# A selective scan with four states of 32 channels in the partitions: dt and dt x through DRAM, y summed in four column groups, two PSUM banks for projections

## The chip, the cores and the metric

The kernel runs on one core of a Trainium2 chip. The core has engines that work side by side, each through its own list of instructions in order: PE (TensorE) multiplies matrices, DVE (VectorE) and POOL (GpSimd) work element by element, ACT (ScalarE) evaluates functions, SP (SyncE) issues most DMA transfers. Semaphores make one engine wait for another. SBUF has 128 partitions; matmuls write into PSUM, which has eight banks of 128 partitions by 2 KB (512 numbers of 32 bits). DRAM lies outside and is reached by DMA alone.

The metric is the device time of one execution in microseconds (us); lower is better.

## The reference, cut to what matters

Two layers on x of shape (2, 2048, 256). Layer 0 adds causal attention and a mixture of experts with a gate; layer 1 adds a selective state-space branch (Mamba) and a linear map with a ternary weight. The change concerns layer 1 and the gate that ends layer 0:

```python
g = sigmoid(concat([abel, moe @ rot]) @ mix_w + mix_b)       # the gate, one number a token
x = residual + abel * (1 - g) + (moe @ rot) * g              # with the attention's share added
xn = layernorm(x)
xs, z = split(xn @ in_proj_w.T, 2)                           # 512 channels each
xs = silu(conv1d(xs, 4 taps) + conv_b)
dt, Bm, C = split(xs @ x_proj_w.T, [16, 32])                 # 16, 16 and 16 wide
dt = softplus(dt @ dt_proj_w.T + dt_proj_b)                  # 512 channels
for t in range(2048):                                        # per channel d and state n (16 states)
    h[d, n] = exp(dt[t, d] * A[d, n]) * h[d, n] + dt[t, d] * Bm[t, n] * xs[t, d]
    y[t, d] = sum_n h[d, n] * C[t, n]
out = x + ((y + xs * D) * silu(z)) @ out_proj_w.T + xn @ ternary(weight).T * alpha + bias
```

The recurrence holds 2 batch rows times 512 channels times 16 states, each a chain of 2048 steps.

## The kernel before, in words

Layer 0 fills the first 2.17 ms or so: projections, attention, routing, `experts`. `rotation`, drawn on beside the experts, computes `rot` and, with `mix_w`, the vector `rw` = rot · mix_w (256 numbers, repeated in all partitions) for the gate. `sab` holds the abel part of the gate, one number a token. Layer 1 and the gate are in `mix_and_state_space`.

The sequence is cut into four chunks of `CH` = 512 tokens; a unit is one chunk of one batch row, eight units in the order (chunk, row). Within a unit the 512 channels lie as `NB` = 4 blocks of 128 in the partitions, with 512 tokens in the free dimension.

The recurrence of a unit runs over 16 states `n`. `product(n)` (L1502 on) loads row n of B and C from DRAM (`bc_d`), repeated over 128 partitions (512 KB), copies B to PSUM on ACT (`bb`, L1507) and multiplies `uh = dx * bb` on DVE (L1509), where `dx` is dt times x. Then for each block m: ACT computes `da = exp(dt * a)` with one `a` a partition (L1526), and DVE runs one scan instruction over the 512 tokens (L1527), started from `carry`. After the four, POOL stores the last column as `carry` (L1532) and multiplies `hh *= C` (L1533). `summed` adds the state's `hh` to `y` on PE with the identity as weights (L1514), into four PSUM banks (`ps_y`) over all 16 states; it is issued for the state before.

Other work of a unit is written as three generators that the recurrence advances at listed places (`places`, pairs of state and block):
- `ahead` of the next unit: normalise (`n`, L1279), transpose (`tr`), project (`in`, L1176), convolve by four diagonal matmuls a block (`cv`, L1316, evacuated as `xs` by ACT, L1325), Silu (L1432), x projection (`xp`), `bc_d` written to DRAM, dt projection, softplus in pieces on ACT, DVE (L1378, L1383) and POOL (L1381), and `dx` (POOL, L1385).
- `behind`: `leave` of the unit before (output projection `out`, L1398 to L1403, added into `xc` by DVE at L1413, stored), then `gate` of this unit (`z` projection, Silu). `gated` for the unit before, at state 1, computes `xs + D` terms with y (DVE, L1460) and multiplies by `zs` (POOL, L1465).
- `mix` of the unit after next: gathers each token's two expert rows (`ys`, POOL's indirect DMA, L1196), scales them on ACT (L1205), adds them (POOL, L1211), multiplies by `rw` (POOL, L1214), reduces on DVE and forms the gate `g` (L1218 to L1224), turns the rows (`moT`), multiplies by `rot` (`pn`, L1241, added by DVE at L1248), adds abel's share on POOL (L1257), and takes the statistics and `r`, `nm` (L1263 to L1270).

`mm`, `issued` and `settle` share one PSUM bank (`ps_m`) among the projections: a matmul group's evacuation is held back and emitted when the next group asks for the bank. `ps_a` has three banks for `da` and `bb`.

The text of the program is not the order of the engines: a scheduler arranges the instructions of each engine by its own estimate of when they are due, and each engine then executes its list in that fixed order. SP's DMA issues stand in such a list too, and one whose source isn't ready holds up those behind it.

Of the kernel before, what the change touches and what calls it, by code (L numbers as in the profile page):

```python
# [19 lines left out]
P = 128  # L20
B = 2
S = 2048
D = 256
# [76 lines left out]
def tile_model(ctx: ExitStack, tc: tile.TileContext, t, out):  # L100
# [54 lines left out]
    rw = keep.tile([P, D], F32, name="rw")  # L155
# [290 lines left out]
def rotation(tc, t, row, ident, ones, pool, ps_pool, tag, rot, rw):  # L446
# [38 lines left out]
    ps = ps_pool.tile([P, D], F32, tag=tag, name="rw_ps")  # L485
    for k in range(2):
        nc.tensor.matmul(
            ps,
            lhsT=mw[:, k : k + 1].to_broadcast([P, P]),
            rhs=turned[:, k, :],  # L490
            start=(k == 0),
            stop=(k == 1),
        )
# [592 lines left out]
def mix_and_state_space(tc, t, col, row, ident, ones, rot, routes, sab, rw, y_d, ab_d, xa_d, out_tiles):  # L1086
# [6 lines left out]

    nc = tc.nc
    NC = S // CH
    QT = CH // P
    full = [P, NB, CH]
    with ExitStack() as ctx:
# [3 lines left out]
        bcp = ctx.enter_context(tc.tile_pool(name="ss_bc", bufs=3))  # L1102
        wk = ctx.enter_context(tc.tile_pool(name="ss_k", bufs=2))
        xcp = ctx.enter_context(tc.tile_pool(name="ss_x", bufs=4))
        dr = ctx.enter_context(tc.tile_pool(name="ss_d", bufs=2, space=DRAM))
        ps_y = ctx.enter_context(tc.tile_pool(name="ss_py", bufs=1, space=PSUM))
        ps_a = ctx.enter_context(tc.tile_pool(name="ss_pa", bufs=3, space=PSUM))
        ps_m = ctx.enter_context(tc.tile_pool(name="ss_pm", bufs=1, space=PSUM))
# [9 lines left out]
        a_neg = w.tile([P, NB * DS], F32, name="a_neg")  # L1118
        nc.scalar.activation(a_neg, col("a_log"), AF.Exp)
        nc.vector.tensor_scalar(a_neg, a_neg, -1.0, None, ALU.mult)  # L1120

# [9 lines left out]
        nc.vector.tensor_scalar(nmb, row("mix_b"), -1.0, None, ALU.mult)  # L1131

# [18 lines left out]
        for b in range(B):  # L1151
            cr = w.tile([P, DS, NB], F32, name=f"carry{b}")
            nc.gpsimd.memset(cr, 0.0)
            carry.append(cr)
            tl = w.tile([P, NB, DC - 1], F32, name=f"tail{b}")
            nc.gpsimd.memset(tl, 0.0)
            tail.append(tl)
# [3 lines left out]
        def settle():  # L1161
            if held:
                take, ps = held.pop()
                take(ps)

        def mm(name, shape=(P, CH)):
            settle()
            return ps_m.tile(list(shape), F32, tag="mm", name=name)

        def issued(ps, take):  # L1170
            held.append((take, ps))
# [13 lines left out]
        def mix(c, b, m_):  # L1185

            u = f"{b}_{c}"
            n0 = (b * NC + c) * QT
            ys = one.tile([P, TOP, QT, D], F32, tag="ys", name=f"ys_{u}")
            ab = one.tile([P, QT, D], F32, tag="ab", name=f"ab_{u}")  # L1190
            nc.sync.dma_start(ab, ab_d[:, n0 : n0 + QT, :])
            xc = m_["xc"] = xcp.tile([P, QT, D], F32, tag="xc", name=f"xc_{u}")
            nc.sync.dma_start(xc, xa_d[:, n0 : n0 + QT, :])
            for i in range(QT):
                for e in range(TOP):
# [6 lines left out]
                    yield  # L1202
            for e in range(TOP):
# [4 lines left out]
                if e == 0:  # L1208
                    yield
# [3 lines left out]

            nc.gpsimd.tensor_tensor(  # L1214
                ys[:, 1], mo, rw.unsqueeze(1).to_broadcast([P, QT, D]), ALU.mult
            )
            g = one.tile([P, 2, QT], F32, tag="g", bufs=2, name=f"g_{u}")
            nc.vector.tensor_reduce(g[:, 0, :], ys[:, 1], AX.X, ALU.add)  # L1218
            nc.vector.tensor_tensor(g[:, 0, :], g[:, 0, :], sab[:, n0 : n0 + QT], ALU.add)
            nc.scalar.activation(g[:, 0, :], g[:, 0, :], AF.Exp, scale=-1.0, bias=nmb)  # L1220
            yield
            nc.vector.tensor_scalar(g[:, 1, :], g[:, 0, :], 1.0, None, ALU.add)
            nc.vector.reciprocal(g[:, 0, :], g[:, 1, :])
            nc.vector.tensor_scalar(g[:, 1, :], g[:, 0, :], -1.0, 1.0, ALU.mult, ALU.add)  # L1224

            moT = ys[:, 1].rearrange("p (k i) d -> p k (i d)", k=2)
            for k in range(2):
# [6 lines left out]
                yield  # L1234
            settle()
# [18 lines left out]
            settle()  # L1254
            for i in range(QT):
                nc.scalar.activation(ab[:, i, :], ab[:, i, :], AF.Copy, scale=g[:, 1, i : i + 1])
            nc.gpsimd.tensor_tensor(xc, xc, ab, ALU.add)  # L1257
# [7 lines left out]
            r = m_["r"] = one.tile([P, QT], F32, tag="r", bufs=3, name=f"r3_{u}")  # L1265
            nc.vector.tensor_scalar(r, mv[:, :, 1], EPS, None, ALU.add)
            nc.scalar.activation(r, r, AF.Sqrt)
            nc.vector.reciprocal(r, r)
            nm = m_["nm"] = one.tile([P, QT], F32, tag="nm", bufs=3, name=f"nm3_{u}")
            nc.vector.scalar_tensor_tensor(nm, mv[:, :, 0], -1.0, r, ALU.mult, ALU.mult)  # L1270
            yield

        def norm(c, b, m_):

            u = f"{b}_{c}"

            n3 = one.tile([P, QT, D], F32, tag="k", name=f"n3_{u}")
            for i in range(QT):
# [4 lines left out]
                    scale=m_["r"][:, i : i + 1],  # L1283
# [23 lines left out]
            m_["xr"] = xr  # L1307

        def convolve(c, b, m_):
            u = f"{b}_{c}"  # L1310
            xr = m_["xr"]
# [19 lines left out]
            nc.gpsimd.tensor_copy(tail[b], xr[:, :, CH:])  # L1331

        def before2(c, b, m_):

            u = f"{b}_{c}"
            xs = m_["xs"]
# [7 lines left out]
            bc_d = m_["bc_d"] = dr.tile([2 * DS, CH], F32, tag="bc_d", name=f"bc_d_{u}")  # L1344

            def out_of(ps):
                nc.scalar.copy(xp, ps)
                nc.sync.dma_start(bc_d, xp[DR:, :])
# [4 lines left out]
            dt = m_["dt"] = two.tile(full, F32, tag="dt", name=f"dt_{u}")  # L1353
# [15 lines left out]
            dx = m_["dx"] = two.tile(full, F32, tag="dx", name=f"dx_{u}")  # L1369
            s1, s2 = dx, one.tile(full, F32, tag="k", name=f"s2_{u}")  # L1370
# [7 lines left out]
            nc.vector.scalar_tensor_tensor(s1, s2, 1.0, s1, ALU.subtract, ALU.subtract)  # L1378
            nc.scalar.activation(s2, s2, AF.Ln)
            yield  # L1380
            nc.gpsimd.tensor_tensor(s2, s2, s1, ALU.subtract)  # L1381
            yield
            nc.vector.scalar_tensor_tensor(dt, dt, 0.0, s2, ALU.max, ALU.add)  # L1383
            yield
            nc.gpsimd.tensor_tensor(dx, dt, xs, ALU.mult)  # L1385
            yield

        def leave(c, b, m_):

            u = f"{b}_{c}"  # L1390
            n0 = (b * NC + c) * QT
            xnT, zs, xc = m_["xnT"], m_["zs"], m_["xc"]
            for h in range(2):
                ps = mm(f"out_{u}_{h}", (P, 2, D))
# [24 lines left out]
        def gate(c, b, m_):  # L1419

            zs = m_["zs"] = one.tile(full, F32, tag="zs", name=f"zs_{b}_{c}")
            for m in range(NB):
# [3 lines left out]
                )  # L1426
                yield
            settle()

        def silu(*tiles):  # L1430
            for x in tiles:
                nc.scalar.activation(x, x, AF.Silu)  # L1432
            yield
# [4 lines left out]
        def ahead(at):  # L1438

            u, m_ = units[at], of[at]  # L1440
            yield from norm(*u, m_)
            yield from convolve(*u, m_)
            yield from silu(m_["xs"])
            yield from before2(*u, m_)

        def behind(at):

            if at > 0:
                yield from leave(*units[at - 1], of[at - 1])
            else:  # L1450
                yield
                yield
            yield from gate(*units[at], of[at])
            yield from silu(of[at]["zs"])

        def gated(m_, pieces):

            xs, y, zs = m_["xs"], m_["y"], m_["zs"]
            for m in range(NB):
# [21 lines left out]
        for kind, at in enumerate(kinds):  # L1481
            for p in at:
                places.setdefault(p, []).append(kind)
# [158 lines left out]
```

## Time and profile before

| | |
|---|---|
| median of three runs | 3504.89 us (3504.43 to 3509.85) |
| profiled execution | 3507.69 us, span 3506.0 us |
| busy share of the span | PE 86%, DVE 63%, ACT 48%, PEld 48%, POOL 32% |
| mean granted PE clock | 0.926 |
| first `uh` of unit 0 | 2271.80 us |
| end of the last scan | 3472.8 us |
| DMA moved | 289.70 MB, mean 83 GB/s |

The profile lists one execution. A row of the groups gives line, engine, operation, output and inputs with their shapes and how many there were; then busy time and the mean duration in ns; then the time that the engine was idle just before them, with what released it. PE runs an fp32 matmul as two passes, so it shows two records for each matmul of the program. PEld is the loading of weights, which overlaps PE. A table by stretches gives each engine's busy time in a window, the granted PE clock (1.0 is full speed) and the share and rate of DMA.

### The profile page before, as it was taken

The page shows a single profiled execution, that of the slowest core. Times are in us where ns is not written, and L with a number is a line of the kernel's source. Part 1 is how long each engine was busy: PE and PEld are TensorE (multiplying, and loading weights), DVE is VectorE, ACT ScalarE, POOL GpSimd, SP SyncE. Part 2 cuts the span into 40 slices and gives each one's busy share as a digit, 9 for nine tenths or more (in the row PEclk, how much of TensorE's full clock was granted, in tenths as well). Part 3 has the DMA queues.
Part 4 walks back from the last instruction along what each step waited for, and adds up shares of the span by engine and source line. Part 5 has one row for each costly group of instructions (what it writes and reads, how often), then busy time and mean ns, then how long its engine had stood idle before and what let it go on. Part 6 is the DMA issues. An engine that isn't in the chain of part 4 may idle for free.

```text
span 3506.0 us, 40686 instructions
## 1 busy us (share of the span) xinstructions
PE 2999.4 (86%) x15574; PEld 1686.0 (48%) x15574; DVE 2218.6 (63%) x2927; ACT 1690.8 (48%) x2423; POOL 1139.4 (32%) x834
## 2 busy tenths in 40 slices
PE   7878899999999998999999995486868787787867
PEld 4633344444444444888888883132423342333423
DVE  6576677777777774331111111298989798889896
ACT  4434455555555554223323323465556565565543
POOL 4223301000100011110010003267566666656664
PEclk9978899999999998999999997697989898888988
DMA  8823213122221104334444431122222222322221
GB/s 296 229 69 79 77 25 49 25 43 37 36 38 25 25 1 154 129 135 146 138 137 145 141 120 45 37 61 68 69 73 67 67 69 65 84 55 60 67 66 48
DMA packets 123874, 289.70 MB, mean 83 GB/s; under 512 B 14464, under 2 KB 57488, under 8 KB 109472
## 3 DMA queue, kind: packets, MB, share of 16 engines
q1 hardware_dynamic: 104960, 187.37, 21.7%
q0 software_dynamic: 17376, 98.58, 8.2%
q8 instruction: 123, 2.02, 0.3%
q10 hardware_dynamic: 1344, 1.16, 0.1%
q14 instruction: 71, 0.58, 0.1%
HBM read 224.13 MB, written 62.91 MB: 82 GB/s over the span
## 4 chain that ended last, share of the span: by engine, by line
PE 49%; DVE 23%; POOL 10%; issue 8%; ACT 7%; DMA 3%; DVEq 0%; POOLq 0%; ACTq 0%; SPq 0%
DVE hh L1527 10%; PE h L1050 8%; PE o L1063 8%; PE pv L661 7%; PE s L703 7%; PE m L606 5%; POOL hh L1533 4%; DVE best L619 4%; DVE uh L1509 4%; PE q L354 3%; PE cv L1316 2%; ACT p L711 2%; DMA x_d<-rows,slots 2%; PE po L751 1%; ACT da L1526 1%
## 5 line engine op out<-in xcount | busy, mean ns | idle before, releaser
L619 DVE TENSOR_REDUCE best<-m 128x2 f32<-128x1024 f32 (+3 forms) x640 | 677.5, 1064 | 161.5 <-PE m L606 152.5
L711 ACT ACTIVATE p<-s 128x1024 f32<-128x1024 f32 (+3 forms) x640 | 573.9, 897 | 418.0 <-PE s L703 399.7
L1527 DVE TENSOR_TENSOR_SCAN hh<-da,carry,uh 128x512 f32<-128x512 f32 x512 | 619.7, 1264 | 84.2 <-PE y L1514 52.5
L1514 PE MATMUL y<-hh,ident 128*128 128x512 f32 x1024 | 531.6, 656 | 86.6 <-POOL hh L1533 68.1
L1533 POOL TENSOR_TENSOR hh<-hh,bc 128x2048 f32<-128x2048 f32 x128 | 579.3, 4526 | 10.4 <-POOL carry L1532 0.2
L1526 ACT ACTIVATE da<-dt,a_neg 128x512 f32<-128x512 f32 x512 | 351.0, 689 | 340.7 <-DVE hh L1527 224.6
L661 PE MATMUL pv<-p,v 128*17 128x256 f32 (+1 forms) x4608 | 412.1, 379 | 46.7 <-POOL p L716 41.9
L716 POOL TENSOR_SCALAR_AFFINE_SELECT p<-p 128x256 f32<-128x256 f32 x256 | 104.6, 410 | 907.4 <-ACT p L711 907.0
L1514 PEld LDWEIGHTS y<-hh,ident 128*128 128x128 f32 x1024 | 205.2, 208 | 363.4 <-issue 235.3
L606 PE MATMUL m<-k,q 64*128 64x512 f32 (+3 forms) x1280 | 322.4, 466 | 9.2 <-DVE best L619 8.4
L703 PE MATMUL s<-q,k 64*128 64x512 f32 (+3 forms) x1280 | 284.9, 410 | 33.2 <-DVE best L619 30.4
L1050 PE MATMUL h<-xT,w 128*128 128x256 f32 x1248 | 294.2, 382 | 1.1 <-DVE xT L1038 1.1
L1057 ACT ACTIVATE hT<-h,b1s 128x256 f32<-128x256 f32 x312 | 142.3, 471 | 314.1 <-PE h L1050 314.1
L1509 DVE TENSOR_TENSOR uh<-dx,bb 128x2048 f32<-128x2048 f32 x128 | 289.4, 2261 | 5.6 <-POOL dx L1385 4.6
L1063 PE MATMUL o<-w,hT 128*128 128x256 f32 x1248 | 280.3, 379 | 0.0
L1020 POOL DMA_INDIRECT w<-in_w,wrow x78 | 76.3, 978 | 621.5 <-PE h L1050 354.1
L703 PE MATMUL s<-tops,onesr 64*128 64x512 f32 (+3 forms) x1280 | 266.9, 379 | 0.0
L606 PEld LDWEIGHTS m<-k,q 64*128 64x128 f32 x1280 | 131.5, 188 | 264.7 <-PE s L703 142.3
L1050 PEld LDWEIGHTS h<-xT,w 128*128 128x128 f32 x1248 | 233.5, 191 | 33.4 <-DVE xT L1038 3.6
L1063 PEld LDWEIGHTS o<-w,hT 128*128 128x128 f32 x1248 | 233.4, 190 | 30.8
L1078 DVE COPY yt<-o 128x512 f32<-128x512 f32 x39 | 27.0, 691 | 336.7 <-PE o L1070 336.7
L661 PEld LDWEIGHTS pv<-p,v 128*17 128x17 f32 x4608 | 86.9, 95 | 246.2 <-POOL p L716 91.6
(298 smaller groups left out, 3690.4 us busy)
## 6 DMA issues: line engine op xcount, KB each, us to landing
bc<-bc_d SPq DMA_DIRECT2D x128, 512.0 KB, 4.9
q<-qk_d SPq DMA_DIRECT2D x128, 128.0 KB, 4.2
k<-qk_d SPq DMA_DIRECT2D x128, 128.0 KB, 7.2
x_d<-zero SPq DMA_DIRECT2D x6, 1664.0 KB
xg<-x_d SPq DMA_DIRECT2D x39, 256.0 KB, 2.8
y_d<-yt SPq DMA_DIRECT2D x39, 256.0 KB
qk_d<-qp SPq DMA_DIRECT2D x16, 512.0 KB, 7.3
qk_d<-kp SPq DMA_DIRECT2D x16, 512.0 KB, 3.9
```

The lines of the kernel that those rows point to most:

```text
L606: nc.tensor.matmul(ps[:, h, 0:n], lhsT=qT[hs, qs], rhs=kT[hs, c * CH : c * CH + n], start=True, stop=True, tile_position=(HP * h, 0),)
L619: nc.vector.tensor_reduce(best[:, i, :, c], ps[:, :, 0:n], AX.X, ALU.max)
L661: nc.tensor.matmul(pv[r0 : r0 + HS + 1, 0, lo - f * HC : HC], lhsT=v[:, b * TPB + kb, 2 * pr + h, :], rhs=pt[:, h, lo:hi], start=False, st ...
L703: nc.tensor.matmul(ps[:, h, off:CH], lhsT=(kT[hs, kb * P : (kb + 1) * P], onesr[hs, :])[i], rhs=(qT[hs, j * CH + off : (j + 1) * CH], tp[h ...
L711: nc.scalar.activation(pt[:, :, off:CH], ps[:, :, off:CH], AF.Exp, scale=float(HS) ** -0.5)
L1050: nc.tensor.matmul(ph, lhsT=w1[:, k * DF + f * P : k * DF + (f + 1) * P], rhs=xT[:, k, :], start=(k == 0), stop=(k == 1),)
L1063: nc.tensor.matmul(po[:, h, :], lhsT=hT[:, f, h * P : (h + 1) * P], rhs=w2[:, f * D : (f + 1) * D], start=(f == 0), stop=False,)
L1509: nc.vector.tensor_tensor(uh, dx, bb.to_broadcast(full), ALU.mult)
L1514: nc.tensor.matmul(y[:, m, :], lhsT=ident, rhs=hh[:, m, :], start=(n == 0), stop=(n == DS - 1))
L1526: nc.scalar.activation(da, dt[:, m, :], AF.Exp, scale=a_neg[:, k : k + 1])
L1527: nc.vector.tensor_tensor_scan(hh[:, m, :], da, uh[:, m, :], carry[b][:, n, m : m + 1], ALU.mult, ALU.add)
L1533: nc.gpsimd.tensor_tensor(hh, hh, cn, ALU.mult)
```

## The change

In the recurrence the 128 partitions hold four states of 32 channels in place of one state of 128 channels. A group (m, g) has channel block m and the states 4g to 4g+3; there are 16 groups (`NU`) a unit, walked block by block, each with four scans, one for each quarter q of the block's channels. So:
- `dt` and dt times x go to DRAM (`dd_d`) in eight DMAs a unit (`spill`) and come back per block m, repeated for the four states, by `decays`: four DMAs of 32 partitions, 512 KB each, into one of two `dd` buffers. Blocks 1 to 3 are asked for while the block before is worked on, block 0 of the next unit at group 14.
- B and C are loaded per g in four DMAs of 32 partitions (`b_and_c`), four times a unit instead of 16; each load serves all four blocks.
- `a_neg` is laid out to match, by 16 small DMAs.
- `summed` adds over the four states in the partitions and over g: with a 128 by 32 selection matrix `sel`, quarter q writes PSUM partitions 32q to 32q+31 (`tile_position`). A block's y is one bank, complete after its four groups; `ps_y` has two banks. `skip` (the D term) and `gated` now work by blocks, when a block's y is there.
- The freed banks go to `ps_m` (two instead of one; `settle` leaves up to one evacuation outstanding) and `ps_a` (four).
- The gate's logit is computed on PE from `moT` and `rw` (now 128 by 2), the sigmoid on ACT with one DVE reciprocal; `nm` moves to POOL, the epsilon of `r` into ACT's bias.
- `places` is written anew, and `uh` has one buffer instead of two.

```diff
-    ps = ps_pool.tile([P, D], F32, tag=tag, name="rw_ps")
-    for k in range(2):
-        nc.tensor.matmul(
-            ps,
-            lhsT=mw[:, k : k + 1].to_broadcast([P, P]),
-            rhs=turned[:, k, :],
-            start=(k == 0),
-            stop=(k == 1),
-        )
+    ps = ps_pool.tile([P, 2], F32, tag=tag, name="rw_ps")
+    for i in range(2):
+        for k in range(2):
+            nc.tensor.matmul(
+                ps[:, i : i + 1],
+                lhsT=turned[:, k, i * P : (i + 1) * P],
+                rhs=mw[:, k : k + 1],
+                start=(k == 0),
+                stop=(k == 1),
+            )
...
+    NU = NB * DS // 4
+    C4 = P // 4
...
-        bcp = ctx.enter_context(tc.tile_pool(name="ss_bc", bufs=3))
-        wk = ctx.enter_context(tc.tile_pool(name="ss_k", bufs=2))
-        xcp = ctx.enter_context(tc.tile_pool(name="ss_x", bufs=4))
+        bcp = ctx.enter_context(tc.tile_pool(name="ss_bc", bufs=4))
+        wk = ctx.enter_context(tc.tile_pool(name="ss_k", bufs=1))
+        xcp = ctx.enter_context(tc.tile_pool(name="ss_x", bufs=3))
         dr = ctx.enter_context(tc.tile_pool(name="ss_d", bufs=2, space=DRAM))
-        ps_y = ctx.enter_context(tc.tile_pool(name="ss_py", bufs=1, space=PSUM))
-        ps_a = ctx.enter_context(tc.tile_pool(name="ss_pa", bufs=3, space=PSUM))
-        ps_m = ctx.enter_context(tc.tile_pool(name="ss_pm", bufs=1, space=PSUM))
+        ps_y = ctx.enter_context(tc.tile_pool(name="ss_py", bufs=2, space=PSUM))
+        ps_a = ctx.enter_context(tc.tile_pool(name="ss_pa", bufs=4, space=PSUM))
+        ps_m = ctx.enter_context(tc.tile_pool(name="ss_pm", bufs=2, space=PSUM))
...
+        a_neg = w.tile([P, 4, NU], F32, name="a_neg")
+        a0 = _COLS["a_log"][0]
+        al = t["cols"].rearrange("(q h) n -> h q n", q=4)
+        for r in range(4):
+            for q in range(4):
+                nc.sync.dma_start(
+                    a_neg[C4 * r : C4 * (r + 1), q, :], al[:, q, a0 + r : a0 + NB * DS : 4]
+                )
+        nc.scalar.activation(a_neg, a_neg, AF.Exp)
         nc.vector.tensor_scalar(a_neg, a_neg, -1.0, None, ALU.mult)
+
+        sel = w.tile([P, C4], F32, name="sel")
+        nc.vector.tensor_reduce(sel, ident.rearrange("p (r c) -> p c r", r=4), AX.X, ALU.add)
...
-        def settle():
-            if held:
-                take, ps = held.pop()
+        def settle(n=0):
+            while len(held) > n:
+                take, ps = held.pop(0)
...
+            settle(1)
...
+            settle(0)
...
-            nc.gpsimd.tensor_tensor(
-                ys[:, 1], mo, rw.unsqueeze(1).to_broadcast([P, QT, D]), ALU.mult
-            )
-            g = one.tile([P, 2, QT], F32, tag="g", bufs=2, name=f"g_{u}")
-            nc.vector.tensor_reduce(g[:, 0, :], ys[:, 1], AX.X, ALU.add)
-            nc.vector.tensor_tensor(g[:, 0, :], g[:, 0, :], sab[:, n0 : n0 + QT], ALU.add)
-            nc.scalar.activation(g[:, 0, :], g[:, 0, :], AF.Exp, scale=-1.0, bias=nmb)
-            yield
-            nc.vector.tensor_scalar(g[:, 1, :], g[:, 0, :], 1.0, None, ALU.add)
-            nc.vector.reciprocal(g[:, 0, :], g[:, 1, :])
-            nc.vector.tensor_scalar(g[:, 1, :], g[:, 0, :], -1.0, 1.0, ALU.mult, ALU.add)
...
+            ps = mm(f"gate_{u}", (P, QT))
+            nc.tensor.matmul(ps, lhsT=ident, rhs=sab[:, n0 : n0 + QT], start=True, stop=False)
+            for i in range(QT):
+                for k in range(2):
+                    nc.tensor.matmul(
+                        ps[:, i : i + 1],
+                        lhsT=moT[:, k, i * P : (i + 1) * P],
+                        rhs=rw[:, k : k + 1],
+                        start=False,
+                        stop=(i == QT - 1 and k == 1),
+                    )
+            g = one.tile([P, 2, QT], F32, tag="g", bufs=2, name=f"g_{u}")
+
+            def sigmoid(ps):
+                nc.scalar.activation(g[:, 0, :], ps, AF.Exp, scale=-1.0, bias=nmb)
+                nc.scalar.activation(g[:, 1, :], g[:, 0, :], AF.Identity, bias=1.0)
+                nc.vector.reciprocal(g[:, 0, :], g[:, 1, :])
+                nc.scalar.activation(g[:, 1, :], g[:, 0, :], AF.Identity, scale=-1.0, bias=1.0)
+
+            issued(ps, sigmoid)
...
+            r = m_["r"] = one.tile([P, 2, QT], F32, tag="r", bufs=3, name=f"r3_{u}")
+            nc.scalar.activation(r[:, 0, :], mv[:, :, 1], AF.Sqrt, bias=eps)
+            nc.scalar.activation(r[:, 1, :], r[:, 0, :], AF.Copy, scale=-1.0)
             nc.vector.reciprocal(r, r)
             nm = m_["nm"] = one.tile([P, QT], F32, tag="nm", bufs=3, name=f"nm3_{u}")
-            nc.vector.scalar_tensor_tensor(nm, mv[:, :, 0], -1.0, r, ALU.mult, ALU.mult)
-            yield
-
-        def norm(c, b, m_):
-
+            nc.gpsimd.tensor_tensor(nm, mv[:, :, 0], r[:, 1, :], ALU.mult)
...
+            dd_d = m_["dd_d"] = dr.tile([NB, C4, 2, 4, CH], F32, tag="dd_d", name=f"dd_d_{u}")
+
+            def spill(i, x):
+                for q in range(4):
+                    nc.sync.dma_start(
+                        dd_d[:, :, i, q, :].rearrange("m h c -> h m c"), x[C4 * q : C4 * (q + 1), :, :]
+                    )
+
+            nc.gpsimd.tensor_tensor(dt, s2, dt, ALU.add)
+            spill(0, dt)
+            yield
+            nc.gpsimd.tensor_tensor(s1, dt, xs, ALU.mult)
+            spill(1, s1)
...
+        def skip(at, m):
+            m_ = of[at]
+            nc.vector.scalar_tensor_tensor(
+                m_["xs"][:, m, :], m_["xs"][:, m, :], col("d")[:, m : m + 1], m_["y"][m], ALU.mult, ALU.add
+            )
+
+        def gated(at, ms):
+            m_ = of[at]
+            nc.gpsimd.tensor_tensor(m_["zs"][:, ms, :], m_["xs"][:, ms, :], m_["zs"][:, ms, :], ALU.mult)
...
+        def behind(at):
+
+            (c, b), m_ = units[at], of[at]
+            if at > 0:
+                skip(at - 1, NB - 1)
+                gated(at - 1, slice(NB - 1, NB))
+                yield
+                yield from leave(at - 1)
+            else:
+                for _ in range(3):
+                    yield
+            skip(at, 0)
+            yield
             zs = m_["zs"] = one.tile(full, F32, tag="zs", name=f"zs_{b}_{c}")
             for m in range(NB):
                 issued(
                     project(NB + m, m_["xnT"], f"z_{b}_{c}_{m}"),
                     lambda ps, m=m: nc.scalar.copy(zs[:, m, :], ps),
                 )
+                if m == 1:
+                    skip(at, 1)
                 yield
             settle()
-
-        def silu(*tiles):
-            for x in tiles:
-                nc.scalar.activation(x, x, AF.Silu)
+            nc.scalar.activation(zs, zs, AF.Silu)
+            yield
+            skip(at, 2)
+            yield
+            gated(at, slice(0, NB - 1))
...
+            [(0, 1), (0, 3), (1, 0), (1, 2), (2, 0), (2, 2), (3, 0), (3, 2), (4, 2), (5, 2), (6, 2)]
+            + [(7, 1), (7, 2), (8, 0), (8, 1), (8, 2), (8, 3), (9, 1), (9, 3), (10, 1), (10, 2)]
+            + [(11, 1), (11, 2), (12, 0), (13, 0)],
+
+            [(1, 1), (4, 0), (5, 0), (5, 1), (9, 0), (9, 2), (10, 0), (10, 3), (12, 1), (13, 1), (14, 1)],
+
+            [(n, q) for n in range(2, 6) for q in (1, 3)]
+            + [(6, 1), (6, 3), (7, 0), (11, 0), (11, 3), (12, 2), (13, 2), (13, 3), (14, 0)]
+            + [(14, 3), (15, 1)],
...
+        def decays(at, m):
+
+            dd = two.tile([P, 2, 4, CH], F32, tag="dd", name=f"dd_{at}_{m}")
+            for r in range(4):
+                nc.sync.dma_start(dd[C4 * r : C4 * (r + 1)], of[at]["dd_d"][m])
+            of[at]["dd", m] = dd
+
+        def b_and_c(at, g):
+
+            bc = bcp.tile([P, 2, CH], F32, tag="bc", name=f"bc_{at}_{g}")
+            for r in range(4):
+                nc.sync.dma_start(
+                    bc[C4 * r : C4 * (r + 1)], of[at]["bc_d"][4 * g + r].partition_broadcast(C4)
+                )
+            of[at]["bc", g] = bc
...
+                m, g = divmod(n, 4)
+                bc = m_["bc", g]
...
+            def summed(n, hh):
+                m, g = divmod(n, 4)
+                if g == 0:
+                    y[m] = ps_y.tile([P, CH], F32, tag="y", name=f"y_{at}_{m}")
+                for q in range(4):
                     nc.tensor.matmul(
-                        y[:, m, :], lhsT=ident, rhs=hh[:, m, :], start=(n == 0), stop=(n == DS - 1)
-                    )
-
-
-            last = y = None
+                        y[m][C4 * q : C4 * (q + 1), :],
+                        lhsT=sel,
+                        rhs=hh[:, q, :],
+                        start=(g == 0),
+                        stop=(g == 3),
+                        tile_position=(0, C4 * q),
...
+                if g == 0 and m + 1 < NB:
+                    decays(at, m + 1)
...
+                if at + 1 < len(units):
+                    if m == NB - 1:
+                        b_and_c(at + 1, g)
+                    if n == 14:
+                        decays(at + 1, 0)
...
-        gated(of[-1], NB)
-        for _ in leave(*units[-1], of[-1]):
+        skip(len(units) - 1, NB - 1)
+        gated(len(units) - 1, slice(NB - 1, NB))
+        for _ in leave(len(units) - 1):
```

## The prediction

> **What bounds the kernel now.** I read the busy shares first, then the slices, the largest groups, the stretches of the second half, and within one stretch the groups and the waits of VectorE; last the end of the run.
>
> The diff touches `mix_and_state_space` (from 2.17 ms on) and a small product ahead of it. The page, busy time and costliest groups:
>
> ```profile
> PE 2999.4 (86%) x15574; PEld 1686.0 (48%) x15574; DVE 2218.6 (63%) x2927; ACT 1690.8 (48%) x2423; POOL 1139.4 (32%) x834
> ...
> L1527 DVE TENSOR_TENSOR_SCAN hh<-da,carry,uh 128x512 f32<-128x512 f32 x512 | 619.7, 1264 | 84.2 <-PE y L1514 52.5
> L1533 POOL TENSOR_TENSOR hh<-hh,bc 128x2048 f32<-128x2048 f32 x128 | 579.3, 4526 | 10.4 <-POOL carry L1532 0.2
> L1509 DVE TENSOR_TENSOR uh<-dx,bb 128x2048 f32<-128x2048 f32 x128 | 289.4, 2261 | 5.6 <-POOL dx L1385 4.6
> ```
>
> PE's 86% is an average over the attention, the experts and this stage. Here the eight units (a chunk of 512 tokens of one batch row each) follow one another; the first `uh` of units 2, 3 and 4 starts at 2564.75, 2725.10 and 2885.41. Engine times of two units:
>
> ```profile
> 2564.75:2725.10 160.35, 124.67 (x293) 55.95 (x292) 139.48 (x109) 93.14 (x133) 103.90 (x48) 0.87 0.26 69
> 2725.10:2885.41 160.31, 124.68 (x293) 56.07 (x292) 139.62 (x109) 93.16 (x133) 103.89 (x48) 0.87 0.28 70
> ```
>
> The columns are PE, PEld, DVE, ACT, POOL, then the granted clock (0.87) and DMA. DVE is busy 139.5 of 160.3: it is the bound, with 20.8 idle. So the change is worth what it does to DVE's work and to its waits. VectorE's groups of the first of these units:
>
> ```profile
> L1527 DVE TENSOR_TENSOR_SCAN hh<-da,carry,uh 128x512 f32<-128x512 f32 x65 | 78.9, 1264 | 11.8 <-PE y L1514 8.2 <-ACT da L1526 2.5
> L1509 DVE TENSOR_TENSOR uh<-dx,bb 128x2048 f32<-128x2048 f32 x16 | 36.2, 2261 | 0.0
> L1270 DVE SCALAR_TENSOR_TENSOR nm<-mv,r 128x4 f32<-128x4 f32 x1 | 3.0, 3007 | 0.0
> L1219 DVE TENSOR_TENSOR g<-g,sab 128x4 f32<-128x4 f32 x1 | 2.8, 2779 | 0.0
> L1222 DVE TENSOR_SCALAR g<-g 128x4 f32<-128x4 f32 x1 | 2.8, 2776 | 0.0
> L1263 DVE BATCH_NORM_STATS2 st<-xc 128x6 f32<-128x256 f32 x4 | 1.5, 406 | 5.6 <-POOL xc L1257 5.6
> L1218 DVE TENSOR_REDUCE g<-ys 128x4 f32<-128x1024 f32 x1 | 1.2, 1220 | 2.5 <-POOL ys L1214 2.5
> ```
>
> **What the change leaves alone.** Sixteen states times four channel blocks become sixteen groups of four states and 32 channels, times four: still 16 `uh` of 2.26, 64 scans of 1.26, 64 `da` of 0.69 and 16 POOL products of 4.5 per unit, of the same shapes.
>
> **What it takes off DVE.** The gate goes to PE and ACT, `nm` to POOL: L1218 1.2, L1219 2.8, L1222 2.8, L1224 0.2, L1266 0.2, L1270 3.0, together 10.2 a unit. Six units carry such a `mix`: −61. ACT (93 of 160) and PE take it up.
>
> **Where the next unit starts.** This decides. In the instruction order of the built program, each engine's list at a unit's end reads:
> - DVE: last scan, `skip` of block 3 (waits for the y sum of the last group), both `xc += out` of `leave`, and only then the next unit's `uh`.
> - ACT: last `da`, `bb`, four copies `xr`, four `xs` from the convolution, table load, Silu, table load, then the next unit's first `da`.
> - PE: y of the last group (waits for POOL's product), `in` 2 and 3, `cv` 0, `out` half 0, `cv` 1, `out` half 1, `cv` 2, `cv` 3.
>
> In the kernel before, the next `uh` stands right behind the last scans (2722.74 + 2.45, then 2725.10), and the next first scan follows 3.0 later. Now it waits for a chain through POOL, PE and ACT. Its pieces can be read at the end of the run, where the same work stands bare:
>
> ```profile
> 3472.93 0.19 POOL L1532 COPY carry<-hh 128x4 f32<-128x4 f32 x1 [2.33 <-DVE hh L1527]
> 3473.20 4.50 POOL L1533 TENSOR_TENSOR hh<-hh,bc 128x2048 f32<-128x2048 f32 x1
> 3477.74 5.40 PE L1514 MATMUL y<-hh,ident 128*128 128x512 f32 x8 [3.39 <-POOL hh L1533]
> 3483.18 2.72 DVE L1460 SCALAR_TENSOR_TENSOR xs<-xs,cols,y 128x512 f32<-128x512 f32 x4 [10.32 <-PE y L1514]
> ...
> 3494.98 1.13 PE L1398 MATMUL out<-tern,xnT 128*128 128x256 f32 x4 [0.78 <-DVE xc L1413]
> ...
> 3500.69 0.69 DVE L1413 TENSOR_TENSOR xc<-xc,out 128x512 f32<-128x512 f32 x1 [5.77 <-PE out L1403]
> ```
>
> POOL's carry and product: 4.8. PE: the y sum is eight passes, warm 0.43 each (3.44). In four column groups I take a third of that. The attention has the same form, groups of up to 32 columns:
>
> ```profile
> 1005.78 0.63 PE L661 MATMUL pv<-p,v 128*17 128x256 f32 x8
> 1006.34 0.51 PE L606 MATMUL m<-k,q 64*128 64x512 f32 x2
> ```
>
> Eight passes of 256 columns in 0.56, 0.07 each, against 0.215 for a full-width pass (half of 0.43): a ratio of 0.33, so 1.1. Bounds: a quarter, and no overlap at all (3.44).
>
> The Trainium skill ("TensorE: Matmul & The Clock Gate", Part 3) gives 2.38 times for three column tiles, which would make the sum 1.45, some 13 us more over the run. "TensorEngine Tiling (Array Packing)", Key Properties, adds that a change of tiling mode drains the engine, which speaks against this edit; the rows above alternate between two tilings and hold such a switch already.
>
> Next on PE: `in` 2 and 3, eight passes, 3.4; four `cv`, 32 passes, 13.8; two `out` halves as at 3494.98 to 3500.69, 11.4. With y 29.7, at the unit's clock of 0.87: 34.1. ACT: `xs` 0.67, table 1.28, Silu 1.91, table 1.28, `da` 0.69: 5.8. From last scan to next scan 44.7, in which DVE does 0.7 + 1.4 + 2.3: idle 40.4. Six boundaries have the whole chain: +242. The seventh has no `ahead`; there `zs`, with one buffer, waits for `out`: POOL 4.8, y 1.3, skip and quarter gate 2.0, `out` 11.6 (13.1 less 1.5 that needs no gate), copies and Silu with tables and `da` 6.4, less DVE's 4.4: +22. In unit 0, too, the first `da` stands behind unit 1's convolution; `in` and `cv` (17.2/0.87) and ACT's 5.8 make 26, of which the first reload (13.8) and `uh` (2.3) cover 16: +10.
>
> **Seams inside a unit.** y of block m ends with group 4m+3, and the order puts `skip` of block m right behind, so DVE meets the same wait three more times: POOL 4.8 + y 1.3 + handover 0.1 = 6.2 at the first, 4.2 at the second and third, where the next `uh` (2.26) or the statistics go first. ACT's scalings of the gathered rows stand among a group's `da`; in the unit before they waited 8.3 for the gather. Between 0 and 8.3 I take half. 18.8 a unit, in units 6 and 7 (no gathers) 3 × 6.2; times eight: +150.
>
> **What goes.** Before's DVE idle from 2271.80 to 3472.8 is 132.7 by the stretches (20.8 in a steady unit: y 8.2, `xc` 5.6, `ys` 2.5, `da` 2.5). It is counted away whole, the waits that take its place being named above: −133. Tail: one quarter is left to gate, both `out` halves have a bank, y is a third: 33.2 becomes about 25: −8.
>
> **Prelude and transfers.** Spill and reload come in front of the first `uh`. 1 MB as `w_in` (6.9) and 2 MB at that rate (13.8): +21. Two PSUM banks take PE's waits for evacuation in 2100 to 2271 (`cv` 3.0, `in` 2.7, `pn` 3.7, `dt` 3.4, `xp` 3.0) at most 15.8, of which I take 13: +8, bounds 0 and +21. In the steady state the reload is hidden: SP's queue puts it behind the third `bc` load, which waits for POOL's product of group 14 (ended 2.6 before the last scan does), and 2 MB at the `bc` rate (512 KB in 4.9) land 20 later, while the `uh` that needs them comes some 37 after the last scan. The spill of dt x behind the first `bc` load has 10 to spare. Should that cover go, each us late costs seven.
>
> The Trainium skill ("SBUF — State Buffer", Door 1) says a transfer into 32 partitions reaches only half of the ports; halving its 436 GB/s, 2 MB would take an estimated 10 us, which changes nothing here; no run yet shows it.
>
> **Sum.** 242 + 22 + 10 + 150 − 133 − 61 − 8 + 8 = +230. The profiled execution took 3507.69 (span 3506.0, 1.7 around it), 0.1% over the median of 3504.89: about 3738, say 3740.
>
> **The rivals.**
> 1. Column groups don't overlap, or PE falls to its cold rate (5.40 for y at 3477.74 instead of 3.70) in the seams: (3.44 − 1.1)/0.87 = 2.7 more at 32 places, +86; with the prelude's +13, 3840. For it: y waits behind an idle PE. Against: the pv rows.
> 2. The reload becomes the bound: two buffers, 2 MB per four groups, 4 × (2.26 + 5.06) = 29 us, so below 74 GB/s. At 60, some 15 MB a unit take 250 against 188, seven times +62: about 4170. For it: 32 partitions a load; `k` (16 partitions, 128 KB) took 7.2. Against: `bc` 107 GB/s, slices at 154.
> 3. Faster: `in`, `cv` and `out` were through PE before the last group's sum. A unit is then 139.5 − 10.2 + 18.8 + boundary; at a boundary of 2.4 that is 150.5 against 160.3, seven times −10 and the prelude: about 3440. It decides below a boundary idle of 12, so PE's 34 would have to be 6. Only `in` 0 and 1 stand ahead in the order.
>
> **Numbers.** Forecast 0.85, rival 1 as far as it lies above the range 0.06, rival 2 0.05, rival 3 0.03, no change 0.01. The measurement tells about 0.2% (7 us) from none. Low end: full clock (−34), no prelude cost (−8), ACT's gather wait gone (−25): 3680. High end: rival 1 and a little contention: 3850. Faster 0.03, same 0.01, slower 0.96.
>
> **What would show it.** Right: from the second unit on about 188 between first `uh`s, DVE busy about 129 of them; DVE's idle before the `xc += out` and first scan of a unit, put down to PE `out` and ACT `da`, some 40; idle before `skip` put down to PE y. Column groups: eight y passes in 1.1 to 1.3. Wrong: a first `uh` right behind scan 15, or idle put down to DMA of `dd`. I'd be most wrong if the boundary chain overlapped better than its order says.

## The result, and the profile after

The changed kernel takes 3762.78 us (median of four, 3762.39 to 3767.97) against 3504.66 of the kernel before in the same runs: ratio 1.074, 95% interval 1.0721 to 1.0759. The forecast was 3740, range 3680 to 3850. The profiled execution has a span of 3760.7, 254.7 more than before.

The page after, busy times and the groups that answer to those shown of before:

```profile
PE 2778.9 (74%) x15722; PEld 1555.6 (41%) x15722; DVE 2155.2 (57%) x2880; ACT 1683.8 (45%) x2441; POOL 1124.3 (30%) x840
...
L1567 PE MATMUL y<-hh,sel 128*32 128x512 f32 x1024 | 239.0, 1025 | 683.4 <-POOL hh L1593 683.3
L1587 DVE TENSOR_TENSOR_SCAN hh<-da,carry,uh 128x512 f32<-128x512 f32 x512 | 617.2, 1265 | 147.1 <-ACT da L1586 134.3
L1593 POOL TENSOR_TENSOR hh<-hh,bc 128x2048 f32<-128x2048 f32 x128 | 577.6, 4513 | 10.3 <-POOL carry L1592 0.4
...
L1559 DVE TENSOR_TENSOR uh<-dd,bb 128x2048 f32<-128x2048 f32 x128 | 292.5, 2286 | 47.8 <-DMA dd<-dd_d 33.5
```

Scans, products and `uh` cost what they did. Every engine has less to do, and the kernel is slower: the loss is idle time. First `uh`s now stand at 2281.36, 2477.59, 2666.35, 2856.22, 3045.12, 3235.10, 3417.39 and 3588.68. Two units (PE, PEld, DVE, ACT, POOL, granted clock, DMA), and what VectorE waited for in the first of them:

```profile
2666.35:2856.22 189.87, 96.48 (x311) 39.17 (x310) 129.70 (x104) 91.85 (x135) 101.72 (x49) 0.67 0.33 81
2856.22:3045.12 188.90, 96.48 (x311) 38.58 (x310) 129.46 (x103) 91.92 (x135) 101.74 (x49) 0.67 0.33 81
```

```profile
DVE xc L1460 <- PE out L1450: 29.9, 3, 13.6
DVE xs L1427 <- PE y L1567: 17.5, 3, 7.0
DVE hh L1587 <- ACT da L1586: 16.4, 4, 10.0
```

A unit takes 189 in place of 160. DVE is busy 9.9 less and idle 60 instead of 20.8. One boundary in the timeline:

```profile
2636.91 0.19 POOL L1592 COPY carry<-hh 128x4 f32<-128x4 f32 x1 [2.55 <-DVE hh L1587]
2637.18 4.50 POOL L1593 TENSOR_TENSOR hh<-hh,bc 128x2048 f32<-128x2048 f32 x1
2641.72 1.94 PE L1567 MATMUL y<-hh,sel 128*32 128x512 f32 x8 [5.38 <-POOL hh L1593]
2643.59 4.42 PE L1194 MATMUL in<-xnT,w_in 128*128 128x512 f32 x8
2643.81 0.75 DVE L1427 SCALAR_TENSOR_TENSOR xs<-xs,cols,y 128x512 f32<-128x512 f32 x1 [6.96 <-PE y L1567]
...
2656.89 0.69 DVE L1460 TENSOR_TENSOR xc<-xc,out 128x512 f32<-128x512 f32 x1 [12.34 <-PE out L1450]
2665.75 0.69 DVE L1460 TENSOR_TENSOR xc<-xc,out 128x512 f32<-128x512 f32 x1 [8.17 <-PE out L1450]
2666.35 2.28 DVE L1559 TENSOR_TENSOR uh<-dd,bb 128x2048 f32<-128x2048 f32 x1
2674.62 1.91 ACT L1360 ACTIVATE xs<-xs 128x2048 f32<-128x2048 f32 x1
...
2678.62 4.81 DVE L1587 TENSOR_TENSOR_SCAN hh<-da,carry,uh 128x512 f32<-128x512 f32 x4 [9.99 <-ACT da L1586]
```

Read the brackets of DVE from top to bottom: y, `out`, `out`, `da`, 37.5 idle between two scans. `uh` computes with nothing that the first three wait for, and the first `da` with nothing of the copies and the Silu that run before it on ACT; they only stand ahead in DVE's and ACT's lists.

### The profile page after: what moved, and what is told of

Its sections match the earlier page's. It is cut to its first block, busy times and chain, and to the rows that moved or that the text cites. A ratio compares the mean times of both kernels' runs of the same rounds, so it can differ in the third digit from the quotient of the medians.

```text
span 3760.7 us, 41396 instructions
## 1 busy us (share of the span) xinstructions
PE 2778.9 (74%) x15722; PEld 1555.6 (41%) x15722; DVE 2155.2 (57%) x2880; ACT 1683.8 (45%) x2441; POOL 1124.3 (30%) x840
## 4 chain that ended last, share of the span: by engine, by line
PE 47%; POOL 18%; issue 17%; DVE 10%; ACT 4%; DMA 3%; SPq 0%; POOLq 0%; ACTq 0%; DVEq 0%
POOL hh L1593 11%; PE o L1064 7%; PE h L1051 7%; PE pv L662 7%; PE s L704 6%; PE m L607 5%; DVE best L620 4%; PE q L354 2%; DVE hh L1587 2%; ACT p L712 2%; PE y L1567 1%; POOL ys L1211 1%; PE in L1194 1%; DMA x_d<-rows,slots 1%; DVE s L1404 1%
## 5 line engine op out<-in xcount | busy, mean ns | idle before, releaser
L1567 PE MATMUL y<-hh,sel 128*32 128x512 f32 x1024 | 239.0, 1025 | 683.4 <-POOL hh L1593 683.3
L1586 ACT ACTIVATE da<-dd,a_neg 128x512 f32<-128x512 f32 x512 | 346.4, 687 | 293.8 <-DVE uh L1559 170.6
L1567 PEld LDWEIGHTS y<-hh,sel 128*32 128x32 f32 x1024 | 25.3, 138 | 862.2 <-POOL hh L1593 852.4
L1559 DVE TENSOR_TENSOR uh<-dd,bb 128x2048 f32<-128x2048 f32 x128 | 292.5, 2286 | 47.8 <-DMA dd<-dd_d 33.5
L704 PE MATMUL s<-q,k 64*128 64x512 f32 (+3 forms) x1280 | 285.7, 411 | 33.5 <-DVE best L620 30.8
L1051 PEld LDWEIGHTS h<-xT,w 128*128 128x128 f32 x1248 | 233.9, 191 | 33.5 <-DVE xT L1039 3.6
L1592 POOL COPY carry<-hh 128x4 f32<-128x4 f32 x128 | 26.1, 204 | 577.1 <-DVE hh L1587 577.1
```

The source lines that it names most:

```text
L704: nc.tensor.matmul(ps[:, h, off:CH], lhsT=(kT[hs, kb * P : (kb + 1) * P], onesr[hs, :])[i], rhs=(qT[hs, j * CH + off : (j + 1) * CH], tp[h ...
L1051: nc.tensor.matmul(ph, lhsT=w1[:, k * DF + f * P : k * DF + (f + 1) * P], rhs=xT[:, k, :], start=(k == 0), stop=(k == 1),)
L1559: nc.vector.tensor_tensor(uh, m_["dd", m][:, 1], bb.to_broadcast(full), ALU.mult)
L1567: nc.tensor.matmul(y[m][C4 * q : C4 * (q + 1), :], lhsT=sel, rhs=hh[:, q, :], start=(g == 0), stop=(g == 3), tile_position=(0, C4 * q),)
L1586: nc.scalar.activation(da, m_["dd", m][:, 0, q, :], AF.Exp, scale=a_neg[:, q, n : n + 1])
```

## The experiments

Theory A: the order that the scheduler chose makes the loss. Against it stand B, that the work of PE, ACT and POOL binds whatever the order; C, that the reload through DRAM binds; and D, that pinning an order is a gain in any kernel.

**Text order.** Ordering edges between instructions of one engine, which add no wait for another, over the whole loop. POOL's and SP's lists are left to the scheduler:

```diff
+        in_order(tc, first, (DVE, Activation, PE))   # each instruction behind the one before it in the text
```

> The changed kernel with one addition: DVE, ACT and PE issue the instructions of the recurrence stage in the order of the program's text (ordering edges, no new waits); loads, tiles and work are the same. Theory A (the loss is made by the order that the scheduler chose): the 38.7 us of idle DVE at a unit boundary shrink to the wait for the first reload, which is issued about 0.7 before the last scan ends and takes some 10 to 15, and the waits before skip mostly go; a unit falls from 190 to about 160, the whole to about 3530 (3490 to 3580). Theory B (the work itself binds: convolution and output projection on PE at its low clock, ACT's tables): the same wait returns at another instruction, unit 180 or more, whole 3700 or more. Theory C (the reload through DRAM binds): the idle time is put down to DMA of dd in every unit and the whole stays over 3650.

3497.5 us, 0.9985 of before (0.9972 to 0.9998): 265 less than the changed kernel, whose loss was 258, so all of the loss is gone. A unit takes 157. VectorE's waits in one unit (its two ends included), and SP's and DVE's side of the boundary:

```profile
DVE uh L1574 <- DMA dd<-dd_d: 21.1, 2, 11.0
DVE st L1308 <- POOL xc L1302: 10.0, 1, 10.0
DVE hh L1602 <- ACT da L1601: 3.2, 3, 1.9
```

```profile
2886.61 1.75 SPq L1535 DMA_DIRECT2D dd<-dd_d  x4
...
2899.61 2.29 DVE L1574 TENSOR_TENSOR uh<-dd,bb 128x2048 f32<-128x2048 f32 x1 [10.10 <-DMA dd<-dd_d]
```

The waits for `out` and Silu are gone from the boundary, and the same work runs beside the scans: B falls. Now C shows, as the next wait in line: the reload lands 13.0 after its issue and costs 10 to 11 a boundary. In the changed kernel's boundary above it was issued at 2636.18, 0.7 before the last scan ended, so by the same 13.0 an estimated 12 of the 37.5 would remain with the load issued there; the longer waits covered them.

**Text order and an early first load, and the early load alone.**

```diff
+                    if n == 13:
+                        decays(at + 1, 0)
                     if m == NB - 1:
                         b_and_c(at + 1, g)
-                    if n == 14:
-                        decays(at + 1, 0)
```

> As the text-order kernel, and block 0 of the next unit is asked for at group 13, ahead of the B and C loads, instead of group 14 behind them. If what is left at the boundary is the first reload's latency: 8 to 10 us less a unit, whole about 3465 (3430 to 3500). If the reload is limited by its rate and not by when it is issued: no more than 2 us less a unit.

> The changed kernel with the early load alone (block 0 asked for at group 13, ahead of the B and C loads), the scheduler's own order kept: the fourth corner beside the changed kernel (3763), text order (3497) and both (3444). In the built program the next unit's uh still stands behind both out additions. Theory A (the order holds the unit's start): within 15 of 3763. Theory C (the first reload's arrival holds it): 60 or more below, as early loading was worth 53 under text order.

With text order 3444.36 (0.9832 of before, 0.9808 to 0.9855), a unit 149; the wait for `dd` falls to 1.6 and 0.7. Alone, under the scheduler's order, 3811.07: not 60 faster but 48 slower than the changed kernel. There the first `da` got ahead of Silu (1.9 idle instead of 10), but `uh` stayed behind both `out` additions, and other waits grew (9.1 for the gate, 6.8 for the statistics). Neither forecast came, 15 around 3763 or 60 below. One moved load let the scheduler list a whole unit anew, so the load's own effect under its order isn't separated here; what is shown is a gain of 53 from it in text order and none without.

**The kernel before in its text order.** The same edit on the kernel before:

```diff
+        in_order(tc, first, (DVE, Activation, PE))
```

> Control: the kernel before with DVE, ACT and PE pinned to its own text order. If pinning is a gain in itself (theory D: the scheduler's order is bad everywhere), it falls below 3480. Theory A expects no gain: the places of the kernel before were listed for work that the scheduler then spread, so text order puts waits for y, POOL and ACT in DVE's list; slower, some 3550 to 3680.

3657.48, ratio 1.0435 (1.0411 to 1.0459). D falls: pinning helps only where `places` was written to be followed. Here 33.6 a unit went to waits for `da`, and 9.9 for the statistics.

**Places tuned.** Text order, the first load at group 12, and in `places`:

```diff
-            + [(11, 1), (11, 2), (12, 0), (13, 0)],
+            + [(11, 1), (11, 2), (11, 3), (12, 1)],
...
-            [(1, 1), (4, 0), (5, 0), (5, 1), (9, 0), (9, 2), (10, 0), (10, 3), (12, 1), (13, 1), (14, 1)],
+            [(1, 1), (4, 0), (5, 0), (5, 1), (9, 0), (9, 2), (10, 0), (10, 3), (12, 1), (13, 3), (14, 1)],
...
-            + [(6, 1), (6, 3), (7, 0), (11, 0), (11, 3), (12, 2), (13, 2), (13, 3), (14, 0)]
-            + [(14, 3), (15, 1)],
+            + [(6, 1), (6, 3), (7, 0), (11, 0), (11, 3), (12, 2), (13, 0), (13, 1), (13, 3)]
+            + [(15, 0), (15, 2)],
```

> As the text-order kernel with the early load, and some places moved: the spill of dt x one group earlier and the first reload at group 12; skip of block 2, the pn sums, the statistics and r a place or more later or earlier, so that each finds its input ready. If what is left of the idle time after the early load is made by single places (first reload, statistics waiting for POOL, skip waiting for y), a unit falls to about 140 with some 10 idle, whole about 3400 (3370 to 3440). If DVE's idle time is set by PE and POOL throughput, it stays at that of the early-load kernel, about 3465.

3413.66, ratio 0.9744 (0.9725 to 0.9764): faster than both kernels, with the changed kernel's layout. The `places` of the kernel before were not tuned for a pinned order, so how much of this gain is the layout's and how much the tuning's is not shown. One unit, and VectorE's waits in it:

```profile
2693.80:2837.65 143.85, 86.23 (x310) 37.70 (x310) 126.28 (x102) 90.87 (x137) 101.77 (x50) 0.76 0.46 107
```

```profile
DVE hh L1602 <- ACT da L1601: 7.3, 5, 3.9
DVE xc L1293 <- PE pn L1286: 4.9, 1, 4.9
DVE xc L1474 <- PE out L1464: 1.5, 1, 1.5
```

**The parts, each undone twice:** in the changed kernel, where DVE has 60 idle a unit, and in the tuned one, where it has under 20.

Full-width sums (`sel` 128 by 128 for each quarter, no `tile_position`):

```diff
-                        y[m][C4 * q : C4 * (q + 1), :],
-                        lhsT=sel,
+                        y[m],
+                        lhsT=sel[:, q, :],
```

> The changed kernel with the y sums at full width: a 128 by 128 selection matrix for each quarter, no column groups; the rest is the same. The sum of a group took 1.94 in the changed kernel. By the forecast's step (column groups take about a third): eight full passes at the low rate seen there (0.85 each) take some 7, so each of the roughly 26 waits before skip that aren't covered grows by 5: whole about 3890 (3810 if PE ran at 0.43 a pass). If column groups bring nothing (they run one after another, and the sum is hidden): within 10 of 3763.

> The tuned-places kernel (3414) with the y sums at full width. In the changed kernel's own order full width cost 35 of an expected 130: the sum took 5.4 instead of 1.94, but the granted clock rose from 0.67 to 0.85 of full speed and the projections of the boundary got through sooner. Theory E (in a good order the sum lies beside other work and the fuller PE keeps its clock): within 20 of 3414. Rival (PE's time becomes the bound, or skip waits by 3.5 a block): 8 units x 4 x 3.5, about 3500 or more.

3797.93 (+35) and 3493.7 (+80). The sum took 5.40 in place of 1.94 at a unit's end of the first:

```profile
2836.60 5.40 PE L1571 MATMUL y<-hh,sel 128*128 128x512 f32 x8 [1.91 <-POOL hh L1596]
2841.83 3.60 PE L1198 MATMUL in<-xnT,w_in 128*128 128x512 f32 x8
...
2854.32 0.69 DVE L1464 TENSOR_TENSOR xc<-xc,out 128x512 f32<-128x512 f32 x1 [11.54 <-PE out L1454]
```

The two times are not at the same granted clock: 0.50 over the 1.94, 0.68 over the 5.40. At 1.00 the sums can be compared, first in the changed kernel, then at full width:

```profile
2703.24 1.07 PE L1567 MATMUL y<-hh,sel 128*32 128x512 f32 x8 [0.83 <-POOL hh L1593]
2627.05 3.70 PE L1571 MATMUL y<-hh,sel 128*128 128x512 f32 x8 [0.70 <-POOL hh L1596]
```

So the column groups take 0.29 of the time. The wait before `skip` at the boundary grew by the 3.4, but `in` ran its eight passes in 3.60 instead of 4.42, and `out` came a little sooner; the granted clock of a unit was 0.83 to 0.85 instead of 0.67. The 3890 expected took every sum at the low clock; about half of the 128 took 3.6 to 3.7, at the full one. The list differs too, so how much of the missing 92 the clock gave back stays open. In the tuned kernel, same order, theory E falls: PE's busy time goes from 86 to 123 a unit, and in a unit DVE's waits for `da` grow from 7.3 to 12.7 and those for `out` from 1.5 to 6.9; the rival named 3500.

One bank for projections:

```diff
-        ps_m = ctx.enter_context(tc.tile_pool(name="ss_pm", bufs=2, space=PSUM))
+        ps_m = ctx.enter_context(tc.tile_pool(name="ss_pm", bufs=1, space=PSUM))
...
-            settle(1)
+            settle(0)
```

> The changed kernel with one PSUM bank for projections instead of two. The forecast counted 13 for the second bank ahead of the first unit and nothing in the steady units: whole about 3776. Rival: on the boundary chain PE must now wait for the evacuation between each convolution and output half, 0.7 to 1 each plus ACT's queue, some 6 to 12 a boundary: whole 3815 to 3860.

> The tuned-places kernel with one PSUM bank for projections. In the changed kernel's order the second bank was worth 150. If that was the bank itself (PE waits 0.7 to 0.8 for each evacuation, some 20 a unit): again 100 or more, 3510 to 3570. If it was the order that the scheduler made with one bank: 20 for the work ahead of the first unit and a few us a unit, 3435 to 3470.

3912.7 (+150) and 3495.74 (+82). With one bank a unit of the changed kernel takes 211.6, one of the tuned kernel 151. Ahead of the first unit the bank is worth 21 and 30 (first `uh` at 2302.3 against 2281.4, 2299.4 against 2269.6), where I counted 13. PE waits 0.68 to 0.84 for each evacuation, on the boundary between all its pieces:

```profile
2910.46 1.98 PE L1194 MATMUL in<-xnT,w_in 128*128 128x512 f32 x4 [0.68 <-ACT xr L1336]
...
2920.39 1.13 PE L1445 MATMUL out<-tern,xnT 128*128 128x256 f32 x4 [0.84 <-ACT xs L1354]
...
2926.85 3.70 PE L1345 MATMUL cv<-xr,taps 128*128 128x512 f32 x8 [0.78 <-DVE xc L1460]
```

The first lies above both of its cases (3776, and 3815 to 3860), the second between its two. In the pinned order the bank is worth 82; what one bank costs beyond that in the changed kernel came with a list that the scheduler made anew, and I did not separate the two there.

The gate back on POOL and DVE:

```diff
+            nc.gpsimd.tensor_tensor(
+                ys[:, 1], mo, rw.unsqueeze(1).to_broadcast([P, QT, D]), ALU.mult
+            )
+            nc.vector.tensor_reduce(g[:, 0, :], ys[:, 1], AX.X, ALU.add)
+            nc.vector.tensor_tensor(g[:, 0, :], g[:, 0, :], sab[:, n0 : n0 + QT], ALU.add)
...
-            ps = mm(f"gate_{u}", (P, QT))
```

> The changed kernel with the gate's logit and sigmoid back on POOL and DVE as before (r and nm stay changed). The forecast counted 7.0 of DVE's time a unit for these (1.2 + 2.8 + 2.8 + 0.2), six units: if that lies on DVE's path, +42, whole about 3805. If it falls into DVE's idle time at the boundaries and seams: within 10 of 3763.

> The tuned-places kernel with the gate back on POOL and DVE. In the changed kernel it cost 6 where 42 was forecast, because DVE had idle time to take it. Here DVE is busy some 88% of a unit: if the 7.0 to 8.0 a unit now lie on its path, six units and the waits for POOL's product ahead of the reduction (2 to 4 each): 3460 to 3490. If they are covered still: within 15 of 3414.

3768.83 (+6; the intervals of the two ratios overlap, so it can't be told from none) and 3448.41 (+35). In the changed kernel DVE's busy time rises by 4.9 a unit and its wait for y falls by 6: the work lies in idle time. With most of the idle time gone the same edit is worth 35 of the 42 forecast, but not as DVE's work: of the 6.3 that a unit grows (143.9 to 150.2) only 1.8 are busy time (126.3 to 128.1) and the rest idle. The gate's addition of `sab`, which takes 2.8 in the kernel before and 3.4 when put back into the changed one, takes 0.16 here.

The gate alone on the kernel before, the same lines the other way round:

```diff
-            nc.vector.tensor_reduce(g[:, 0, :], ys[:, 1], AX.X, ALU.add)
...
+            ps = mm(f"gate_{u}", (P, QT))
...
+            issued(ps, sigmoid)
```

> One part alone on the kernel before: the gate's logit on PE and its sigmoid on ACT with one DVE reciprocal (one bank, r and nm as before). DVE is the bound there with 139.5 of 160.3 a unit; if the 7.0 are on its path: six units, -42, whole about 3463. If the place of the work sets DVE's waits instead (ACT and PE reach the gate later, the scheduler lists things anew): within 15 of 3505.

3493.54, ratio 0.9967 (0.9954 to 0.9979): 10 of 42. DVE's waits in two units before, then in two units with the gate moved:

```profile
DVE hh L1527 <- PE y L1514: 16.3, 4, 4.8
```

```profile
DVE hh L1538 <- PE y L1525: 31.0, 8, 8.4
```

DVE gave back 7.4 a unit at the scans that wait for y to free an `hh` buffer.

## Why the prediction was right

The sign, the mechanism and the size came out as forecast (+230 against +258); the text-order run shows that the order of the engines' lists is the cause. By the terms of the sum, idle time of DVE as the trace names it:

| term | forecast | measured |
|---|---|---|
| six boundaries | +242 | 228 (37.3 to 38.7 each, forecast 40.4) |
| seventh boundary | +22 | 26 |
| unit 0's start | +10 | 11 |
| seams inside units | +150 | 156 |
| idle time of the kernel before | −133 | −133 (its own trace) |
| DVE's work taken off | −61 | −53 (busy 1068 to 1016, first `uh` to last scan) |
| tail | −8 | −11 |
| prelude | +8 | +9.6 |

The named waits sum to 421 against 424. The forecast is 25 short of the trace because DVE's work shrank by 8 less and because some 20 of idle time in pieces that no wait names (441 by window less busy time, 421 named) were in no term.

Inside the terms not all was right.
- *Boundary.* From last scan to next scan 41.8 passed, forecast 44.7. I divided PE's 29.7 by the unit's clock; in fact `in`, `cv` and `out` took 29.0, because after two slow passes PE ran at 0.43 a pass through the whole chain. The y sum, at the low rate, took 1.9 instead of 1.3.
- *Column groups.* At one clock the ratio is 0.29 (1.07 to 3.70), taken as 0.33. The sign that was named, eight passes in 1.1 to 1.3, came in ten of the 128 sums; 118 took 1.94, at half the clock. Rival 1 had PE's low rate right (granted clock 0.67 instead of 0.87), but groups that overlap make that cost little.
- *First seam.* Forecast 6.2 idle; it cost 0.4. I read that `skip` stands behind the group's scans, and overlooked what the softplus piece ahead of it does beside POOL's product: it takes 6.6 instead of 2.3 and covers the wait, which is so paid as busy time (the kernel before paid it too: 6.4). The second and third seam cost more than 4.2 (6.05, and 4.5 + 1.6), unit 0 29.5 rather than 18.8, so the sum held by luck as well as by working.
- *Gate.* The work taken off lies in DVE's busy time, but hardly in the kernel's: the gate's 42 of the 61, undone, cost 6, no clear difference; `nm` and `r`, the other 19, were not undone. The forecast counted boundary idle and DVE's work as additive, which a removal inside a unit full of waits is not.
- *Second bank.* "Two PSUM banks" were given 13, in the prelude. They are worth 150 in this order and 82 in a good one.
- *Reload.* Hidden, as forecast: DVE waits for `dd` once, in the prelude (33.5, forecast 21 for spill and load). In the text-order run 2 MB landed in 13.0 (161 GB/s), forecast 13.8 to 20. Rival 2 needed under 74 GB/s (by its own 29 us it is 72). The page of the Trainium skill "SBUF — State Buffer" (Door 1) would give an estimated 10; the measured 13.0 doesn't contradict its rule, and no run here compares it with a transfer of the same size into 128 partitions.
- *Rival 3* named what had to hold for a gain, a boundary idle under 12: with 10 to 11 in text order the kernel fell just below the one before.
- *Low end.* Its three parts take 67 off 3738, which is 3671 and not 3680; the result lies far from either.

## What to carry to other kernels

Read the order that was built, not only the program: where a scheduler arranges the lists, a hand-written interleaving is a proposal, and an instruction that waits for another engine costs what everything behind it on its engine loses. A change of layout can be good and measure badly; before judging it, look for waits whose consumer doesn't need what is waited for, and pin the order in one run. And the value of a part is only defined beside its surroundings: moving the gate off the bounding engine was worth 6, no clear difference, where that engine had 60 idle a unit, and 35 where it had under 20.

## What was not expected of the hardware

- PE's granted clock followed how densely PE was used: 0.67 in the changed kernel's units, where it sat idle 5.4 before each y sum, 0.83 to 0.85 with the longer full-width sums, 0.87 in the tuned kernel with them and 0.76 without. The Trainium skill ("TensorE: Matmul & The Clock Gate", the table under "Why this matters for your kernels") says that an idle gap of more than about 3 us drops the clock to half; gaps of 5.4 and passes at half rate agree.
- Shortening PE's sums to three tenths thus slowed what followed them: `in` took 4.42 instead of 3.60 for its eight passes.
- An operation of DVE over 128x2048, the softplus piece, took 6.3 to 6.7 beside POOL's product and 2.3 in the text-order run, where it stood clear of it. In one unit of the changed kernel the product ran from 2518.13 to 2522.63 and the piece from 2518.32 to 2524.79: it ended 2.2, about its own time, after the product.
